# A spiking-rate recommender on one core: last step by pieces, the table's partial part moved forward, two blocks stored in halves, splits finished one copy later

## The chip, the cores and the metric

The kernel runs on one core of one Trainium2 chip. The metric is the time of one execution on the device in microseconds (us). Before the change the median of 3 runs is 1647.41 us (1646.87 to 1650.15). The profile is one further execution, which took 1574.98 us.

## The reference, cut to what matters

A batch of 1024 sequences of 50 item numbers looks up rows of 128 numbers in a table of 100,001 items (row 0 counts as zero). The running mean of the rows is normalised over the batch at each step, drives a leaky spiking unit for 50 steps, and the mean spike count is multiplied by the whole table.

```python
e = emb[seq]                                   # 1024 x 50 x 128
prefix = jnp.cumsum(e, axis=1)
uF = prefix / jnp.minimum(t_idx, lengths)      # t_idx = 1..50
y = (uF - mean) * rsqrt(var + 1e-5) * gamma + beta     # mean, var over the batch
# 50 times: v = v + (x - v)/2; spike = v >= 1; v = v - spike
scores = spikes.mean(axis=0) @ emb.T           # 1024 x 100001, float32
```

The output alone is 1024 x 100,001 x 4 bytes = 409.6 MB.

## The kernel before, in words

**Stage one: 50 steps.** Everything is kept with the 128 features on the partitions and the 1024 sequences along the free axis. GpSimd (POOL) gathers the rows of step t+1 with 8 indirect DMAs of 128 rows each (`gather`, L195). TensorE (PE) transposes the eight blocks of step t into two PSUM banks, `pre[0]` and `pre[1]`, where the running sum builds up (L307). VectorE (DVE) scales each half of 512 columns (L316) and takes its statistics (L317), joins them (L327), and works out the normalising factor in five small instructions (L340 to L346), with a square root on ScalarE (ACT, L331) between. ACT applies the factor (`x`, L350), DVE subtracts half of what is left of the old state (`step`, L353), and PE sums the spikes by a matmul with the identity (`counted`, L275). In the last step (t = 49) the state is made in three groups of 128, 512 and 384 columns (L378), and each group's spikes are added to the count so far (`spiked`, L286), which gives `countA`, `countB` and `countC`, the left operands of stage two. A row of 16 idle transposes (`warm`, L376) keeps PE going meanwhile.

**Stage two: scores.** The table is cut into 98 parts of 1024 items; the last one, part 97, has 673. A part is read as rows (`fetch`, L99), transposed by PE into PSUM (`turned`, L128), and split into a rounded copy `hi` by ACT (L150) and the remainder `lo` by DVE (L151): `prepare`. `product` (L155) multiplies one of eight count blocks n (128 sequences each) with `hi` and `lo`. DVE and ACT take turns at copying the results out of PSUM with the factor 1/50 (L467, L469), and SyncE (SP) stores them (`store`, L167).

The parts are worked on in chunks: `WIDTHS` gives 4 chunks of 2 parts, 4 of 3, 11 of 6 and 3 of 4. Within a chunk, the loop runs over n = 0 to 7 and then over the chunk's parts, so that one pair (chunk, n) is a block that is stored with one DMA, of 1024, 1536, 3072 or 2048 KB. The output tiles `o` have four places in chunks 0 to 3 and three afterwards (`turns`, L432, L436, L440); a block can be written only when the store that last used its place has landed. PSUM holds four tiles of 1024 columns (`ps`, L410), shared by products and transposed parts in order of use.

The next chunk's parts are prepared inside the current one: `ready()` (L445) is called after the blocks n = 2 to 6 (L478) and after each part of block 7 (L475), and prepares one part if there is a place for it. Chunk 0 is special: its block n = 0 is made ahead of the loop (L394 to L404), and its block n = 1 is stored part by part (L471).

The first 38 parts are read in stage one by SP; the others are read by ACT's queue, three parts at a time, in the chunks from number 8 on, after the blocks n = 1 and n = 4 (L481). Part 97 is the last one read there: a DMA of its 5 full groups of 128 rows (L115), 512 bytes to a packet, and one of the 33 rows that are left (L120).

Nothing reorders the program: every engine works in the order in which the code issues. The build gives the DMAs of SP and ACT eight completion semaphores in turn, in the order of the code, and each DMA waits, on the engine that issues it, for the DMA eight before it.

Of the kernel before, what the change touches and what calls it, by code (L numbers as in the profile page):

```python
# [20 lines left out]
P = 128  # L21
# [15 lines left out]
def rec_kernel(  # L37
# [35 lines left out]

    parts = -(-N // HALF)
    assert sum(WIDTHS) == parts
    rows = {}
    split = {}

    free = [
        [embp.tile([P, HALF], F32R, tag=f"{x}{i}", name=f"{x}_{i}") for x in ("hi", "lo")] for i in range(2)  # L80
    ]

    def size(q):
        return min(HALF, N - q * HALF)
# [14 lines left out]
    def fetch(r, q, n):  # L99

        engine = nc.sync if q < HELD else nc.scalar
        k = slot(q)[1]
        n = min(n, parts - q)
        whole = n - (size(q + n - 1) < HALF)
        if whole:
            engine.dma_start(
                out=r[:, k : k + whole, :],
                in_=table[q * HALF : (q + whole) * HALF, :].rearrange("(q p k) d -> p q (k d)", p=P, k=KQ),
            )
        if whole < n:  # L110
            full, rest = divmod(size(parts - 1), P)
            c1 = (parts - 1) * HALF
            r = r[:, k + whole, :].rearrange("p (k d) -> p k d", d=D)
            if full:
                engine.dma_start(  # L115
                    out=r[:, :full, :],
                    in_=table[c1 : c1 + full * P, :].rearrange("(k p) d -> p k d", p=P),
                )
            if rest:
                engine.dma_start(out=r[:rest, full, :], in_=table[c1 + full * P : N, :])  # L120

    def turned(q, pt):
        r = rows.pop(q)
# [18 lines left out]
    def prepare(q, pt):  # L142
        turned(q, pt)
        split[q] = hi, lo = free.pop(0)
        hw = size(q)
        if hw % 2:
            nc.vector.memset(hi[:, hw : hw + 1].bitcast(F32), 0.0)
            nc.vector.memset(lo[:, hw : hw + 1].bitcast(F32), 0.0)
        vp, vh, vl = views(q, pt, hi, lo)
        nc.scalar.copy(vh, vp)  # L150
        nc.vector.tensor_tensor(vl, vp, vh.bitcast(F32), ALU.subtract)  # L151

    def product(po, q, n, k0, kw):  # L155
        kw += kw % 2
        for j, part in enumerate(split[q]):
            nc.tensor.matmul(  # L158
                po[:, :kw],
                lhsT=counts[n],  # L160
                rhs=part[:, k0 : k0 + kw],
                start=j == 0,
                stop=j == 1,
            )
# [5 lines left out]
    with ExitStack() as ph:  # L170
# [23 lines left out]

        def gather(t):  # L195
            es[t] = gp.tile([P, B], F32, tag="e", name=f"e_{t}")
            for n in range(NB):
                nc.gpsimd.indirect_dma_start(  # L198
                    out=es[t][:, n * P : (n + 1) * P],
                    out_offset=None,  # L200
                    in_=table,
                    in_offset=bass.IndirectOffsetOnAxis(ap=idx[:, n, t : t + 1].bitcast(U32), axis=0),
                )
# [81 lines left out]
        def spiked(out, cs, v):  # L285
            nc.vector.scalar_tensor_tensor(out, v, V_TH, count[:, cs], ALU.is_ge, ALU.add)  # L286

        whole = slice(0, B)
        halves = [slice(h * BANK, (h + 1) * BANK) for h in range(B // BANK)]
        v = None  # L290
# [3 lines left out]
        for t in range(T):  # L294
            last = t == T - 1
            if t + 1 < T:
                gather(t + 1)
            e = es.pop(t)
            if last:
                s = lp.tile([P, B], BF16, tag="s", name=f"s_{t - 1}")  # L300
                nc.vector.tensor_single_scalar(s, v, V_TH, ALU.is_ge)
                nc.vector.tensor_tensor(negv, s, v, ALU.subtract)
            uF = up.tile([P, B], F32, tag="uF", name=f"uF_{t}")
            bs = sp.tile([P, B // BANK, 6], F32, tag="bs", name=f"bs_{t}")
            for h, cs in enumerate(halves):
                for k in range(0, BANK, P):
                    nc.tensor.matmul(  # L307
                        pre[h][:, k : k + P],
                        lhsT=e[:, h * BANK + k : h * BANK + k + P],
                        rhs=ident,  # L310
                        start=False,
                        stop=last,
                        is_transpose=True,
                        skip_group_check=True,
                    )
                nc.vector.scalar_tensor_tensor(uF[:, cs], rlen[:, cs], 1.0 / (t + 1), pre[h], ALU.max, ALU.mult)  # L316
                nc.vector.bn_stats(bs[:, h, :], uF[:, cs])  # L317
            if not last:
                correct(t + 1, l)
            else:  # L320

                counted(t - 1, s)
# [4 lines left out]
            nc.vector.bn_aggr(mv, bs.rearrange("p h s -> p (h s)"))  # L327


            r = sp.tile([P, 1], F32, tag="r", name=f"r_{t}")  # L330
            nc.scalar.activation(r, mv[:, 1:2], AF.Sqrt, bias=eps)  # L331
            nc.scalar.activation(uF, uF, AF.Identity, bias=mv[:, 0:1], scale=-1.0)


            if t and not last:
                s = lp.tile([P, B], BF16, tag="s", name=f"s_{t - 1}")
                nc.vector.tensor_single_scalar(s, v, V_TH, ALU.is_ge)  # L337
                counted(t - 1, s)

# [12 lines left out]
            def step(vt, cs):  # L352
                nc.vector.scalar_tensor_tensor(vt, negv[:, cs], -0.5, vt, ALU.mult, ALU.add)  # L353

            if not last:
                vt = vp.tile([P, B], F32, tag=f"v{t % 2}", name=f"v_{t}")
                x(vt, whole)
                if t:
                    nc.vector.tensor_tensor(negv, s, v, ALU.subtract)
# [18 lines left out]
        groups = [  # L378
            (slice(0, P), pre[0][:, :P], countA),
            (slice(P, P + BANK), pre[1], countB),  # L380
            (slice(P + BANK, B), vC, countC),
        ]
# [40 lines left out]
    for c, W in enumerate(WIDTHS):  # L423
# [30 lines left out]
        for n in range(NB):  # L454
# [2 lines left out]
            pool, tag, most = turns[blocks % len(turns)]  # L457
            blocks += 1
            o = pool.tile([P, most * HALF], F32, tag=tag, name=f"o_{c}_{n}")
            for q in range(q0, q1):  # L460
                h0 = (q - q0) * HALF
                hw = size(q)
# [2 lines left out]
                    product(po[:, k0 : k0 + BANK], q, n, k0, min(BANK, hw - k0))  # L465
                if turn % 2 == 0:
                    nc.vector.tensor_scalar_mul(o[:, h0 : h0 + hw], po[:, :hw], 1.0 / T)  # L467
                else:
                    nc.scalar.mul(o[:, h0 : h0 + hw], po[:, :hw], 1.0 / T)  # L469
# [39 lines left out]
```

## Time and profile before

| what | value |
|---|---|
| median of 3 runs | 1647.41 us |
| profiled execution: its time, its span | 1574.98 us, 1573.2 us |
| first gather to end of the last | 4.2 to 503.6 us |
| first store of scores issued | 511.62 us |
| last store of scores issued | 1561.15 us |
| busy: PE, DVE, ACT, POOL | 1147.9, 942.1, 630.6, 378.5 us |
| HBM read, written | 77.69 MB, 409.60 MB |
| mean granted TensorE clock | 0.966 |

A busy time is what an engine spent in its instructions; issuing a DMA doesn't count. The second part of the page cuts the span into 40 slices of 39.3 us and gives the busy share of each engine and of the 16 DMA engines together. The chain of waits follows the run back from its end, at each step to what released it. A group's row gives its line, engine, operation, shapes and count, then the busy time and mean duration, then how long its engine sat idle before it and what ended that. The rows of DMA issues give the median time from issue to landing, which is the time at which the last of the 16 DMA engines has finished its share. The profiled execution is 72.4 us shorter than the median of the runs; no view says where that lies.

### The profile page before, as it was taken

How to read it: one execution, taken by the hardware profiler on the slowest of the kernel's cores; microseconds unless marked ns; L12 is line 12 of the kernel's file. 1: busy time of each engine (PE TensorE's matmuls, PEld its weight loads, DVE VectorE, ACT ScalarE, POOL GpSimd, SP SyncE). 2: the span in 40 equal slices, each digit the busy share in tenths (PEclk: the TensorE clock that was granted, in tenths of full speed). 3: DMA queues.
4: the chain of work that ended last, by engine and by line, in shares of the span. 5: the costliest groups of instructions: out<-in, count | busy, mean ns of one | idle time of the engine just before them, and what ended most of it. 6: DMA issues, size and time to landing. Idle time of an engine off the chain costs nothing.

```text
span 1573.2 us, 12601 instructions
## 1 busy us (share of the span) xinstructions
PE 1147.9 (73%) x4538; PEld 817.6 (52%) x4548; DVE 942.1 (60%) x1161; ACT 630.6 (40%) x700; POOL 378.5 (24%) x406
## 2 busy tenths in 40 slices
PE   4555555555555998889878878887888778777885
PEld 2222222222233776668667666666666667665763
DVE  4777777777777665667555545545555555554553
ACT  2322222222233554555444444444444444443442
POOL 6777777777776000000000000000000000000000
PEclk9999999999999999999999999999999999999998
DMA  9622222222221999999999999999999999999898
GB/s 338 247 53 53 53 53 52 53 53 53 53 79 45 385 416 403 423 417 402 426 429 428 430 427 424 421 415 428 418 428 423 414 428 410 426 424 426 362 423 371
DMA packets 54859, 488.14 MB, mean 310 GB/s; under 512 B 12139, under 2 KB 12940, under 8 KB 32524
## 3 DMA queue, kind: packets, MB, share of 16 engines
q1 hardware_dynamic: 33424, 429.81, 65.1%
q0 software_dynamic: 12800, 26.24, 6.3%
q10 hardware_dynamic: 8572, 31.28, 5.0%
q8 instruction: 36, 0.59, 0.1%
q14 instruction: 27, 0.22, 0.0%
HBM read 77.69 MB, written 409.60 MB: 310 GB/s over the span
## 4 chain that ended last, share of the span: by engine, by line
DMA 50%; POOL 19%; PE 11%; issue 10%; ACT 5%; DVE 4%; another core or an unknown queue 0%; DVEq 0%; ACTq 0%; SPq 0%; POOLq 0%
DMA scores<-o 46%; POOL e L198 19%; PE po L158 10%; ACT o L469 4%; DMA e<-in_L_rec_emb_table,idx 3%; DVE o L467 2%; DMA rows<-in_L_rec_emb_table 2%; PE pt L128 1%; PE pre L307 0%; ACT pairs L150 0%; DVE s L337 0%; DVE bs L317 0%; DVE uF L316 0%; DVE pairs L151 0%; DMA idx<-in_r_seq 0%
## 5 line engine op out<-in xcount | busy, mean ns | idle before, releaser
L467 DVE TENSOR_SCALAR o<-po 128x1024 f32<-128x1024 f32 x391 | 464.1, 1220 | 354.3 <-DMA scores<-o 314.5
L469 ACT ACTIVATE o<-po 128x1024 f32<-128x1024 f32 (+1 forms) x391 | 388.1, 1019 | 548.9 <-DMA scores<-o 336.2
L198 POOL DMA_INDIRECT e<-in_L_rec_emb_table,idx x400 | 377.8, 945 | 124.5 <-issue 116.4
L158 PE MATMUL po<-pairs,countB 128*128 128x512 f32 x1136 | 304.6, 415 | 69.0 <-ACT o L469 52.1
L158 PEld LDWEIGHTS po<-pairs,countB 128*128 128x128 f32 x1136 | 218.5, 197 | 132.0 <-ACT o L469 66.8
L307 PE MATMUL pre<-ident,e 128*128 128x128 f32 x400 | 156.2, 452 | 152.4 <-DMA e<-in_L_rec_emb_table,idx 149.0
L158 PE MATMUL po<-pairs,countC 128*128 128x512 f32 x852 | 230.4, 416 | 49.3 <-ACT o L469 49.3
L158 PEld LDWEIGHTS po<-pairs,countC 128*128 128x128 f32 x852 | 163.6, 198 | 94.2 <-ACT o L469 60.5
L307 PEld LDWEIGHTS pre<-ident,e 128*128 128x128 f32 x400 | 79.2, 200 | 246.1 <-DMA e<-in_L_rec_emb_table,idx 223.6
L151 DVE TENSOR_TENSOR pairs<-pt,pairs 128x1024 fp32r<-128x1024 f32 x71 | 86.3, 1222 | 91.3 <-ACT pairs L150 91.2
L331 ACT ACTIVATE r<-mv,eps 128x1 f32<-128x1 f32 x50 | 14.7, 295 | 305.5 <-DVE mv L327 305.5
L316 DVE SCALAR_TENSOR_TENSOR uF<-rlen,pre 128x512 f32<-128x512 f32 x100 | 68.4, 684 | 108.3 <-PE pre L307 108.2
L128 PE MATMUL pt<-ident,rows 128*128 128x128 f32 x782 | 111.7, 290 | 9.7 <-ACT o L469 5.1
L128 PEld LDWEIGHTS pt<-ident,rows 128*128 128x128 f32 x782 | 100.3, 152 | 29.9 <-issue 8.8
L158 PE MATMUL po<-hi,countB 128*128 128x512 f32 x216 | 89.5, 414 | 15.8 <-ACT o L469 12.6
L264 PE MATMUL pre<-zT,l 128*128 128x512 f32 x100 | 78.1, 783 | 18.9 <-DVE uF L316 18.8
L275 PE MATMUL sums<-s,ident_h 128*128 128x512 bf16 x88 | 45.4, 607 | 60.6 <-DVE s L337 60.6
L158 PE MATMUL po<-lo,countB 128*128 128x512 f32 x216 | 86.5, 402 | 0.0
L158 PE MATMUL po<-pairs,countA 128*128 128x512 f32 x284 | 71.7, 395 | 9.3 <-ACT o L469 9.2
L150 ACT CAST pairs<-pt 128x1024 fp32r<-128x1024 f32 x71 | 71.8, 1012 | 15.0 <-PE pt L128 14.8
L158 PE MATMUL po<-hi,countC 128*128 128x512 f32 (+1 forms) x162 | 67.8, 418 | 11.7 <-ACT o L469 11.7
L350 ACT ACTIVATE v<-uF,hgb,a 128x1024 f32<-128x1024 f32 x49 | 59.2, 1208 | 37.6 <-DVE a L346 37.5
(76 smaller groups left out, 841.9 us busy)
## 6 DMA issues: line engine op xcount, KB each, us to landing
scores<-o SPq DMA_DIRECT2D x88, 3072.0 KB, 20.3
scores<-o SPq DMA_DIRECT2D x32, 1536.0 KB, 8.9
scores<-o SPq DMA_DIRECT2D x16, 2048.0 KB, 12.6
scores<-o SPq DMA_DIRECT2D x30, 1024.0 KB, 8.6
rows<-in_L_rec_emb_table ACTq DMA_DIRECT2D x19, 1536.0 KB, 29.3
rows<-in_L_rec_emb_table SPq DMA_DIRECT2D x6, 3072.0 KB, 25.3
scores<-o SPq DMA_DIRECT2D x8, 1872.5 KB, 11.3
e<-in_L_rec_emb_table,idx POOLq DMA_INDIRECT x400, 2.5
```

The lines of the kernel that those rows point to most:

```text
L128: nc.tensor.transpose(pt[:, k0 : k0 + kw], r[:kw, k0 : k0 + D], ident[:kw, :kw])
L150: nc.scalar.copy(vh, vp)
L151: nc.vector.tensor_tensor(vl, vp, vh.bitcast(F32), ALU.subtract)
L158: nc.tensor.matmul(po[:, :kw], lhsT=counts[n], rhs=part[:, k0 : k0 + kw], start=j == 0, stop=j == 1,)
L198: nc.gpsimd.indirect_dma_start(out=es[t][:, n * P : (n + 1) * P], out_offset=None, in_=table, in_offset=bass.IndirectOffsetOnAxis(ap=idx[: ...
L264: nc.tensor.matmul(pre[h], lhsT=l, rhs=zT[:, h * BANK : (h + 1) * BANK], start=t == 0, stop=False, skip_group_check=True,)
L275: nc.tensor.matmul(sums[h], lhsT=ident_h, rhs=s[:, h * BANK : (h + 1) * BANK], start=t == 0, stop=t == T - 2, skip_group_check=True,)
L307: nc.tensor.matmul(pre[h][:, k : k + P], lhsT=e[:, h * BANK + k : h * BANK + k + P], rhs=ident, start=False, stop=last, is_transpose=True, ...
L316: nc.vector.scalar_tensor_tensor(uF[:, cs], rlen[:, cs], 1.0 / (t + 1), pre[h], ALU.max, ALU.mult)
L350: nc.scalar.activation(vt, uF[:, cs], AF.Identity, bias=hgb[:, 1:2], scale=a)
L467: nc.vector.tensor_scalar_mul(o[:, h0 : h0 + hw], po[:, :hw], 1.0 / T)
L469: nc.scalar.mul(o[:, h0 : h0 + hw], po[:, :hw], 1.0 / T)
```

## The change

**Last step by pieces.** In the last step block 4 (columns 512 to 639) is gathered last, and the step is worked in pieces of 512, 384 and 128 columns instead of two halves. The sums for the earlier spikes (`counted`) move ahead of the last piece's transposes. The old state `negv` is made in three parts, each placed between other work. In all steps one of the five small DVE instructions goes, and another, `ve`, is placed where DVE waits for the square root. `warm` uses the other PSUM tile.

**The partial part.** `order` puts parts 96 and 97 at places 2 and 3, so that they form chunk 1 (1697 columns) and are read in stage one; the last chunk is now 4096 columns wide where it was 3745.

**Halves.** In chunk 8, the first with 6 parts, the blocks n = 0 and 1 are stored after 3 parts and again after 6.

**The split one copy later.** `prepare` no longer issues DVE's subtraction. It is issued by `finish()`, after DVE's next copy out of PSUM, or ahead of a product that needs it. In chunk 0, `ready()` is called from n = 4 on and no longer from n = 2.

```diff
+    order = [0, 1, parts - 2, parts - 1, *range(2, parts - 2)]
...
+    def column(q):
+        return order[q] * HALF
...
         nc.scalar.copy(vh, vp)
-        nc.vector.tensor_tensor(vl, vp, vh.bitcast(F32), ALU.subtract)
+        unsplit.append((q, vp, vh, vl))
+
+    def finish():
+        while unsplit:
+            _, vp, vh, vl = unsplit.pop(0)
+            nc.vector.tensor_tensor(vl, vp, vh.bitcast(F32), ALU.subtract)

     def product(po, q, n, k0, kw):
         kw += kw % 2
+        if any(u[0] == q for u in unsplit):
+            finish()
...
-            for n in range(NB):
+            order = list(range(NB))
+            if t == T - 1:
+                order.append(order.pop(NB // 2))
+            for n in order:
...
+        thirds = [slice(0, P), slice(P, P + BANK), slice(P + BANK, B)]
+
+        def negated(cs):
+            nc.vector.tensor_tensor(negv[:, cs], s[:, cs], v[:, cs], ALU.subtract)
...
-                nc.vector.tensor_tensor(negv, s, v, ALU.subtract)
...
+            pieces = halves if not last else halves[:1] + [slice(B - 3 * P, B), slice(BANK, BANK + P)]
+            bs = sp.tile([P, len(pieces), 6], F32, tag="bs", name=f"bs_{t}")
+            for j, cs in enumerate(pieces):
+                h = cs.start // BANK
+                if last and j == len(pieces) - 1:
+                    counted(t - 1, s)
...
+            ve = sp.tile([P, 1], F32, tag="ve", name=f"ve_{t}")
+            nc.vector.tensor_scalar_add(ve, mv[:, 1:2], BN_EPS)
...
+            if last:
+                negated(thirds[0])
             nc.vector.reciprocal(r, r)
             q = sp.tile([P, 1], F32, tag="q", name=f"q_{t}")
-            nc.vector.tensor_mul(q, r, r)
-            nc.vector.scalar_tensor_tensor(q, mv[:, 1:2], BN_EPS, q, ALU.add, ALU.mult)
+            nc.vector.scalar_tensor_tensor(q, r, ve, r, ALU.mult, ALU.mult)
...
-        warm = vp.tile([P, HALF], F32, tag="v0", name="warm")
+        warm = vp.tile([P, HALF], F32, tag="v1", name="warm")
...
+        negated(thirds[1])
         for cs, vt, _ in groups:
             x(vt, cs)
         cs, vt, first = groups[0]
         step(vt, cs)
         spiked(first, cs, vt)
+        negated(thirds[2])
...
                 if turn % 2 == 0:
                     nc.vector.tensor_scalar_mul(o[:, h0 : h0 + hw], po[:, :hw], 1.0 / T)
+                    finish()
...
-                if c == 0 and n == 1:
-                    store(n, q * HALF, o[:, h0 : h0 + hw])
                 if n == NB - 1:
                     free.append(split.pop(q))
                     ready()
-            if c or n > 1:
-                store(n, q0 * HALF, o[:, : min(N, q1 * HALF) - q0 * HALF])
-            if 2 <= n < NB - 1:
+                if q + 1 == q1 or c == 0 and n == 1 or c == MIDDLE and n < 2 and (q + 1 - q0) % 3 == 0:
+                    store(n, column(q0) + done, o[:, done : h0 + hw])
+                    done = h0 + hw
+            if (2 if c else 4) <= n < NB - 1:
                 ready()
```

`fetch` is rewritten so that it reads neighbouring full parts with one DMA, and the partial one with the two DMAs that it had. The first group of six parts, one DMA before, now takes five: parts 0 and 1, part 96, the two of part 97, and parts 2 and 3.

More of the change, by code (lines that the diff above doesn't have):

```diff
@@ L75, in rec_kernel @@
     assert sum(WIDTHS) == parts
+    order = [0, 1, parts - 2, parts - 1, *range(2, parts - 2)]
     rows = {}
     split = {}
+    unsplit = []
     free = [
@@ L81, in rec_kernel @@
     ]
+    def column(q):
+        return order[q] * HALF
     def size(q):
-        return min(HALF, N - q * HALF)
+        return min(HALF, N - column(q))
     def slot(q):
@@ L101, in fetch @@
         engine = nc.sync if q < HELD else nc.scalar
[L102 to L114, printed above, removed]
+        end = min(q + n, parts)
+        while q < end:
+            k, c0, n = slot(q)[1], column(q), 1
+            if size(q) == HALF:
+                while q + n < end and column(q + n) == c0 + n * HALF and size(q + n) == HALF:
+                    n += 1
                 engine.dma_start(
-                    out=r[:, :full, :],
-                    in_=table[c1 : c1 + full * P, :].rearrange("(k p) d -> p k d", p=P),
-                )
-            if rest:
-                engine.dma_start(out=r[:rest, full, :], in_=table[c1 + full * P : N, :])
+                    out=r[:, k : k + n, :],
+                    in_=table[c0 : c0 + n * HALF, :].rearrange("(q p k) d -> p q (k d)", p=P, k=KQ),
+                )
+            else:
+                full, rest = divmod(size(q), P)
+                part = r[:, k, :].rearrange("p (k d) -> p k d", d=D)
+                if full:
+                    engine.dma_start(
+                        out=part[:, :full, :],
+                        in_=table[c0 : c0 + full * P, :].rearrange("(k p) d -> p k d", p=P),
+                    )
+                if rest:
+                    engine.dma_start(out=part[:rest, full, :], in_=table[c0 + full * P : N, :])
+            q += n
     def turned(q, pt):
@@ L301, in rec_kernel @@
                 nc.vector.tensor_single_scalar(s, v, V_TH, ALU.is_ge)
-                nc.vector.tensor_tensor(negv, s, v, ALU.subtract)
             uF = up.tile([P, B], F32, tag="uF", name=f"uF_{t}")
-            bs = sp.tile([P, B // BANK, 6], F32, tag="bs", name=f"bs_{t}")
-            for h, cs in enumerate(halves):
-                for k in range(0, BANK, P):
+            pieces = halves if not last else halves[:1] + [slice(B - 3 * P, B), slice(BANK, BANK + P)]
[4 more added lines that the diff above has]
+                    counted(t - 1, s)
+                for c0 in range(cs.start, cs.stop, P):
+                    k = c0 - h * BANK
                     nc.tensor.matmul(
                         pre[h][:, k : k + P],
-                        lhsT=e[:, h * BANK + k : h * BANK + k + P],
+                        lhsT=e[:, c0 : c0 + P],
                         rhs=ident,
@@ L315, in rec_kernel @@
                     )
-                nc.vector.scalar_tensor_tensor(uF[:, cs], rlen[:, cs], 1.0 / (t + 1), pre[h], ALU.max, ALU.mult)
-                nc.vector.bn_stats(bs[:, h, :], uF[:, cs])
+                nc.vector.scalar_tensor_tensor(
+                    uF[:, cs],
+                    rlen[:, cs],
+                    1.0 / (t + 1),
+                    pre[h][:, cs.start - h * BANK : cs.stop - h * BANK],
+                    ALU.max,
+                    ALU.mult,
+                )
+                nc.vector.bn_stats(bs[:, j, :], uF[:, cs])
             if not last:
@@ L320, in rec_kernel @@
             else:
-                counted(t - 1, s)
                 count = once.tile([P, B], F32, tag="zT", name="count")
@@ L358, in rec_kernel @@
                 if t:
-                    nc.vector.tensor_tensor(negv, s, v, ALU.subtract)
+                    negated(whole)
                 step(vt, whole)
@@ L377, in rec_kernel @@
         vC = vp.tile([P, B - BANK - P], F32, tag="v1", name="vC")
[L378 to L382, printed above, removed]
+        groups = list(zip(thirds, (pre[0][:, :P], pre[1], vC), (countA, countB, countC)))
+        negated(thirds[1])
         for cs, vt, _ in groups:
@@ L459, in rec_kernel @@
             o = pool.tile([P, most * HALF], F32, tag=tag, name=f"o_{c}_{n}")
+            done = 0
             for q in range(q0, q1):
@@ L467, in rec_kernel @@
                     nc.vector.tensor_scalar_mul(o[:, h0 : h0 + hw], po[:, :hw], 1.0 / T)
+                    finish()
                 else:
```

## The prediction

> **What bounds the kernel now.** I read the page's slices and chain first, then the waits of SP's queue, then the stretches in which the DMA engines are not full, in windows of 1 us.
>
> ```profile
> PE   4555555555555998889878878887888778777885
> DMA  9622222222221999999999999999999999999898
> DMA 50%; POOL 19%; PE 11%; issue 10%; ACT 5%; DVE 4%; another core or an unknown queue 0%; DVEq 0%; ACTq 0%; SPq 0%; POOLq 0%
> L198 POOL DMA_INDIRECT e<-in_L_rec_emb_table,idx x400 | 377.8, 945 | 124.5 <-issue 116.4
> ```
>
> There are two stages. Up to about 504 us POOL issues 400 gathers, 0.945 us each with some 0.3 us between them: 400 x 1.25 = 499 us, without a break. Nothing that DVE saves in the first 49 steps counts, because POOL sets their pace. From 512 us on the DMA engines are full, while PE shows 7 to 9 tenths and DVE (60% of the span) has room too. So the change can gain in three places: between the last gather and the first store, in gaps of the stores, and at the end.
>
> The gaps look like this. The last two columns are the share of the 16 DMA engines and GB/s.
>
> ```profile
> 521.00:522.00 1.00, 1.00 (x6) 0.83 (x5) 1.00 (x2) 0.64 (x1) 0.00 (x0) 1.00 0.07 25
> ...
> 713.00:714.00 1.00, 1.00 (x6) 0.80 (x5) 1.00 (x2) 0.25 (x1) 0.00 (x0) 1.00 0.21 86
> ```
>
> ```profile
> 1457.00:1458.00 1.00, 1.00 (x4) 0.80 (x3) 0.56 (x1) 0.41 (x1) 0.00 (x0) 0.50 0.32 135
> ...
> 1460.00:1461.00 1.00, 1.00 (x6) 0.82 (x5) 0.82 (x2) 0.51 (x1) 0.00 (x0) 1.00 0.09 34
> 1461.00:1462.00 1.00, 1.00 (x11) 0.93 (x9) 0.58 (x1) 0.73 (x1) 0.00 (x0) 1.00 0.04 16
> ```
>
> Added up as 1 minus the share, the gap from 1453 to 1463 is 6.3 us, the one around 713 to 719 about 2 us, and the start (512 to 522) 2.1 us. The big one has a clear cause in SP's waits and in the landing times of the reads:
>
> ```profile
> SPq L167 <- DMA rows<-in_L_rec_emb_table: 26.7, 3, 13.1
> ```
>
> ```profile
> rows<-in_L_rec_emb_table ACTq DMA_DIRECT2D x19, 1536.0 KB, 29.3
> ...
> rows<-in_L_rec_emb_table ACTq DMA_DIRECT2D x1, 320.0 KB, 50.7
> ```
>
> The read of part 97 takes 50.7 us to land where a read of three full parts takes 29.3. Eight completion semaphores go round among SP's and ACT's DMAs, so the store eight DMAs later waits for it, up to 13.1 us, with all later stores behind it on SP.
>
> But a gap in the mean share is not yet lost time. At 1460 to 1462 the share is 0.09 and 0.04, and one engine of 16 is 0.06: about one engine is still working, while the other fifteen have run out. ACT's copies, which start when a store has fully landed, show whether that last engine ever paused:
>
> ```profile
> 1453.79 1.94 ACT L469 ACTIVATE o<-po 128x1024 f32<-128x1024 f32 x2 [5.66 <-DMA scores<-o]
> ...
> 1464.14 1.02 ACT L469 ACTIVATE o<-po 128x1024 f32<-128x1024 f32 x1 [0.94 <-DMA scores<-o]
> ...
> 1469.81 1.94 ACT L469 ACTIVATE o<-po 128x1024 f32<-128x1024 f32 x2 [2.04 <-DMA scores<-o]
> ...
> 1474.89 1.94 ACT L469 ACTIVATE o<-po 128x1024 f32<-128x1024 f32 x2 [1.86 <-DMA scores<-o]
> ```
>
> From 1453.79 to 1474.89, 21.1 us, four stores of 2048 KB land (one of them releases DVE, at 1458.95). Undisturbed, three such stores take 15.2 us (issues at 1487.42 and 1502.59 in the chain), 5.07 each, so four take 20.3. The slowest engine lost at most 0.8 us in a gap of 6.3. At 713 it is the same: ACT's waits for landings at 709.61 and 743.90 are 34.3 us apart, and three stores of 1536 KB (3.86 each, from the waits at 701.87, 705.75 and 709.61) and three of 3072 KB (7.52, from 743.90, 751.39 and 758.95) make 34.1. The stage is bound by one DMA engine that lags behind the others; the gaps are the others waiting for it.
>
> **What the Trainium skill says.** "DMA: Bandwidth & Descriptors", section "Why a DMA increments its semaphore by 16 and not by 1": up to 16 engines finish a DMA independently, and only the full count means that it has landed. The trace agrees: places come free at an even pace although 15 engines idle. The same page, "Queues, rings and completion order": each engine serves its queues in turn, packet by packet. That explains the 50.7 us: many packets of 512 bytes, each behind a long packet of a store. "VectorE: DVE Perf Modes", section "The TRN2 errata": a fixed cost for each instruction. Here a DVE instruction takes 0.30 us on 128 columns, 0.56 on 384 and 0.69 on 512, so that pieces cost more in all but end sooner.
>
> **The change part by part, against the profiled execution (1574.98 us, span 1573.2).**
>
> *Last step.* DVE's rows before:
>
> ```profile
> 506.55 0.69 DVE L317 BATCH_NORM_STATS2 bs<-uF 128x6 f32<-128x512 f32 x1
> 507.28 0.21 DVE L327 BATCH_NORM_AGGREGATE mv<-bs 128x2 f32<-128x12 f32 x1
> ...
> 518.75 1.23 DVE L151 TENSOR_TENSOR lo<-pt,hi 128x1024 fp32r<-128x1024 f32 x1 [1.40 <-ACT hi L150]
> ```
>
> The last gather feeds PE at 505.31; after that 0.67 + 0.69 are needed on 512 columns, in future 0.30 + 0.30 on 128. DVE reaches the last piece at about 506.0, having done 502.13 + 1.22 (spikes) + 0.68 + 0.69 + 0.56 + 0.55 and the pauses, so the aggregate starts at about 506.65: 0.65 earlier. `ve` (0.16) and `negated(thirds[0])` (0.30) exceed the 0.36 wait for the square root by 0.14; one instruction less gives 0.19 back: 0.0. `negated(thirds[1])`, about 0.65, lies in an idle 0.59 ahead of `step`, where only ACT's copies were awaited: 0.13 late. So `countA` and the first store (511.62) come 0.5 earlier. `negated(thirds[2])`, 0.55, stands ahead of `countB`: 0.65 - 0.13 - 0.55 and the pauses leave `countB` 0.1 to 0.2 later than before. Moving `counted` forward (two matmuls, 1.06) fits in PE's wait for the last gather. POOL issues the same 8 gathers. In all other steps POOL's 1.25 x 8 covers everything.
>
> *Chunk 0 without a split at n = 2.* Between its blocks 2 and 3 go eight transposes (1.03), ACT's copy (1.01), and on DVE 1.40 of waiting and 1.23 of subtraction. Block 3's store came at 521.17, 3.3 us after block 2's; without the split PE's 1.85 us for a block sets it, at about 519.3. The gap 521 to 522 (0.93) closes. All engines were idle there, so this is real. With the 0.5 at the first store, less what returns at 515 and 518 because `countB` is no earlier: 1.15 in all (bounds 0.3 and 1.7). The two splits now come at n = 4 and 7, when two stores of 2.5 us are queued.
>
> *Partial part.* The stall goes. Gain for the slowest engine: 0 to 0.8, I take 0.3. Stage two reads 351 more rows, 180 KB, 0.4 us at 420 GB/s, less the dearer small packets: 0.2 lost. Five DMAs for one at the start lie on an SP that is otherwise idle until 444 us; POOL waited 3.0 us in 10 times in all for gathers to land. Chunk 1 writes 351 columns less and the last one more: 0.
>
> *Halves.* PE and DVE deliver the first half 2 us sooner, but the slowest engine did not lack work. Two DMAs of 1536 KB cost 7.72 for 7.52: 0.2 lost for each of two blocks, bounds 0 and 0.4; I take 0.3.
>
> *Split one copy later.* DVE's wait for ACT, 91.3 us over 71 splits, moves behind a copy. The price: a transposed part keeps one of four PSUM tiles longer, and when the copy waits for a place in `o`, the subtraction (1.23) now waits too, and PE with it. In a block with two splits that is some 1.5 us more, against 7.7 from a free place to the store in the longest case (1027.85 to 1035.45). Two more stores of 7.5 us are queued meanwhile, 15 us. So 0. If that cover were gone, every such block would cost up to 1.5.
>
> Sum: -1.15 - 0.3 + 0.2 + 0.3 = -0.95 us. The profile would become 1574.0. The median is 72.4 us above the profiled time, and no view says where; I carry the difference over as it is: 1647.4 - 0.95 = 1646.5 us.
>
> **The rivals.** *The gaps count in full*: 6.0 at 1453, 1.8 at 713, 1.15 at the start, less 0.5: -8.45, 1639.0 us. For it: the share of the page's slices, and the runs may not share the profile's one slow engine. Against it: the even landings. *The last step does not get shorter*, because the last piece waits for PSUM or for `counted`, and the start gains nothing: 0.2, 1647.6 us. *Starved by the later subtraction*: in the 11 chunks of 6 parts, block 7 takes its splits behind its copies. It decides when the path from a free place to the store exceeds the 15 us that are queued; at 0.5 us beyond it, 11 x 0.5 - 0.95 = +4.55, 1652.0 us. Against it: 7.7 + 1.5 is well below 15.
>
> **How the numbers follow.** Forecast 0.57, last step not shorter 0.16, gaps in full 0.19, starved 0.08. About 0.2% (3.3 us) is what a measurement of this kernel can tell from no change. The forecast (bounds 1645 to 1648) and the second rival lie within it; the first rival lies beyond it, from 1644 down to 1637; the last is slower. That gives faster 0.19, same 0.73, slower 0.08. The range 1640.0 to 1649.3 takes in the first two and half of the first rival.
>
> **What would show it.** The first store at about 511.1 and no gap at 521; no wait of SP for rows; after the split's move, longer idle of DVE ahead of L467 but none of the DMA queue. If I am right, the lag persists: the fifteen faster engines idle in small gaps or at the end instead, and the stores land at the same pace. If the landings from 1453 on come 5 us earlier than the start alone explains, the first rival is right. If windows of 1 us show low shares at the end of each chunk of 6 parts, the last is.

## The result, and the profile after

| | median | lowest to highest | runs |
|---|---|---|---|
| before | 1648.26 us | 1646.87 to 1650.15 | 4 |
| after | 1648.68 us | 1646.67 to 1650.16 | 4 |

The ratio is 1.0001, with a 95% interval from 0.9984 to 1.0018: no difference that can be measured. The profiled execution of after took 1650.16 us, its span is 1648.0 us. It can't be laid straight beside the profile of before (1574.98 us), because, as the experiments below suggest, the two come from chips on which stage one takes different times; the record names no chip for either. So I read stage one and stage two separately.

The page of after first: busy shares of PE and granted clock in 40 slices, DMA share, the chain, POOL's gathers.

```profile
PE   4343433334343498988988788887888888887884
PEclk7555555555555589999999989999999999999998
DMA  9511111111112179999999999999999999999998
DMA 38%; PE 19%; DVE 16%; another core or an unknown queue 9%; POOL 6%; ACT 6%; issue 5%; DVEq 0%; ACTq 0%; SPq 0%; POOLq 0%
L217 POOL DMA_INDIRECT e<-in_L_rec_emb_table,idx x400 | 378.6, 946 | 184.6 <-issue 114.3
```

POOL is no longer the chain's second entry (19% before, 6% here). Its gathers cost what they did, but it sits idle for 184.6 us between them instead of 124.5. The last gather starts at 563.5 us instead of 502.7, and the first store is issued at 583.9 instead of 511.6: the 72 us lie in stage one. From the first store to the end it is 1064.1 us here, and 1061.6 in the profile of before. Stage two didn't become shorter, it became longer.

Next the waits of SP's queue (us in total, times, longest): the longest in total, and the only one that a DMA ends:

```profile
SPq L183 <- DVE o L507: 875.4, 176, 11.1
SPq L546 <- DMA scores<-o: 11.8, 3, 4.9
```

The waits for rows (26.7 us before) are gone; what is left is the wait for the last stores at the end. And the windows of 1 us, with the DMA share and GB/s last. The first and third lie as long after the first store as the gaps at 521 and 713 did; the fourth and fifth answer to those from 1457 on:

```profile
593.00:594.00 1.00, 1.00 (x9) 0.92 (x8) 0.12 (x1) 1.00 (x2) 0.00 (x0) 1.00 1.08 451
645.00:646.00 1.00, 1.00 (x3) 0.78 (x3) 0.00 (x0) 0.67 (x1) 0.00 (x0) 0.50 0.08 33
785.00:786.00 1.00, 1.00 (x6) 0.83 (x5) 1.00 (x2) 0.67 (x1) 0.00 (x0) 1.00 1.04 442
1528.00:1529.00 1.00, 1.00 (x6) 1.00 (x5) 0.25 (x1) 0.05 (x1) 0.00 (x0) 0.50 0.23 98
1535.00:1536.00 1.00, 1.00 (x9) 0.91 (x7) 0.00 (x0) 1.00 (x2) 0.00 (x0) 1.00 0.16 66
```

The gaps that the change aimed at are closed (shares 1.08 and 1.04; a little above 1 occurs in this view). In their place stands a new one at 645, with TensorE's clock at 0.50, and gaps late in the stage remain.

### The profile page after: what moved, and what is told of

The parts are those of the page before. It is cut to its first block, busy times and chain, and to the rows that moved or that the text cites. A ratio compares the mean times of both kernels' runs of the same rounds, so it can differ in the third digit from the quotient of the medians.

```text
span 1648.0 us, 12648 instructions
## 1 busy us (share of the span) xinstructions
PE 1114.5 (68%) x4548; PEld 827.3 (50%) x4548; DVE 941.6 (57%) x1165; ACT 636.2 (39%) x700; POOL 379.3 (23%) x406
## 4 chain that ended last, share of the span: by engine, by line
DMA 38%; PE 19%; DVE 16%; another core or an unknown queue 9%; POOL 6%; ACT 6%; issue 5%; DVEq 0%; ACTq 0%; SPq 0%; POOLq 0%
DMA scores<-o 37%; PE po L174 17%; POOL e L217 6%; ACT o L510 5%; DVE bs L356 3%; DVE uF L348 3%; DVE v L393 2%; DVE s L376 2%; DVE negv L311 2%; PE pt L136 2%; DVE o L507 2%; DMA e<-in_L_rec_emb_table,idx 1%; DVE a L386 0%; DVE mv L364 0%
## 5 line engine op out<-in xcount | busy, mean ns | idle before, releaser
L507 DVE TENSOR_SCALAR o<-po 128x1024 f32<-128x1024 f32 x391 | 469.9, 1221 | 475.4 <-DMA scores<-o 326.8
L510 ACT ACTIVATE o<-po 128x1024 f32<-128x1024 f32 (+1 forms) x391 | 394.0, 1020 | 546.0 <-PE po L174 319.1
L217 POOL DMA_INDIRECT e<-in_L_rec_emb_table,idx x400 | 378.6, 946 | 184.6 <-issue 114.3
L174 PE MATMUL po<-pairs,countB 128*128 128x512 f32 x1136 | 308.2, 417 | 74.2 <-ACT o L510 59.6
L283 PEld LDWEIGHTS pre<-zT,l 128*128 128x128 f32 x100 | 27.8, 279 | 289.6 <-issue 176.5
L348 DVE SCALAR_TENSOR_TENSOR uF<-rlen,pre 128x512 f32<-128x512 f32 (+1 forms) x101 | 68.2, 675 | 168.6 <-remote 152.1
L136 PE MATMUL pt<-ident,rows 128*128 128x128 f32 x782 | 108.0, 283 | 12.1 <-ACT o L510 8.3
L339 PE MATMUL pre<-ident,e 128*128 128x128 f32 x400 | 102.7, 422 | 18.4 <-DMA e<-in_L_rec_emb_table,idx 14.3
L136 PEld LDWEIGHTS pt<-ident,rows 128*128 128x128 f32 x782 | 96.3, 147 | 31.3 <-ACT o L510 12.8
L339 PEld LDWEIGHTS pre<-ident,e 128*128 128x128 f32 x400 | 85.5, 223 | 50.9 <-issue 25.3
L294 PE MATMUL sums<-s,ident_h 128*128 128x512 bf16 x98 | 49.6, 608 | 75.4 <-DVE s L376 45.5
```

Source lines behind the costliest of these rows:

```text
L136: nc.tensor.transpose(pt[:, k0 : k0 + kw], r[:kw, k0 : k0 + D], ident[:kw, :kw])
L174: nc.tensor.matmul(po[:, :kw], lhsT=counts[n], rhs=part[:, k0 : k0 + kw], start=j == 0, stop=j == 1,)
L217: nc.gpsimd.indirect_dma_start(out=es[t][:, n * P : (n + 1) * P], out_offset=None, in_=table, in_offset=bass.IndirectOffsetOnAxis(ap=idx[: ...
L283: nc.tensor.matmul(pre[h], lhsT=l, rhs=zT[:, h * BANK : (h + 1) * BANK], start=t == 0, stop=False, skip_group_check=True,)
L294: nc.tensor.matmul(sums[h], lhsT=ident_h, rhs=s[:, h * BANK : (h + 1) * BANK], start=t == 0, stop=t == T - 2, skip_group_check=True,)
L339: nc.tensor.matmul(pre[h][:, k : k + P], lhsT=e[:, c0 : c0 + P], rhs=ident, start=False, stop=last, is_transpose=True, skip_group_check=True,)
```

## The experiments

The runs were made in four groups, each on one chip, which I call A to D. The kernel before was timed along with each group:

| chip | kernel before, median | lowest to highest | runs |
|---|---|---|---|
| A | 1647.76 us | 1639.57 to 1649.27 | 31 |
| B | 1574.88 us | 1574.53 to 1575.82 | 16 |
| C | 1647.73 us | 1639.69 to 1650.00 | 43 |
| D | 1574.62 us | 1574.20 to 1575.39 | 25 |

### Where the 72 us are (chip A)

**The kernel before, unchanged.**

> The kernel before, unchanged, profiled again. Theory A (the 72 us that the first profiled execution lacked are lost in stage one, whatever the change, because TensorE runs there below its full clock in nearly every execution): span about 1645 us, gathers until about 562 us instead of 504, POOL idle about 60 us more than in the first profile, TensorE completing transposes 0.43 us or more apart instead of 0.21. Rival (the change itself lengthened stage one by 60 us and gained as much in stage two): a span of 1645 us with stage one ending at 504 and a longer stage two.

Measured: 1647.87 us, ratio 1.0002 (0.9984 to 1.0020). Its profiled execution has a span of 1647.0 us, the last gather at 563.3, the first store at 584.3. In this respect before and after are alike; the rival falls. The change has nothing to do with the 72 us. One sign that I had named is missing: at a clock of 0.50 the transposes start 0.21 us apart (eight in 1.91 us), not 0.43. Whether TensorE's clock has to do with the 72 us is the next question.

**Idle matmuls** in stage one, to keep TensorE busy, two ahead of each transpose and, in a second kernel, three:

```diff
+            spare = vp.tile([P, B], F32, tag=f"v{t % 2}", name=f"spare_{t}")
...
+                    for _ in range(2):
+                        nc.tensor.matmul(spare[:, :BANK], lhsT=ident_h, rhs=ones, start=True, stop=True)
                     nc.tensor.matmul(
                         pre[h][:, k : k + P],
```

> The kernel after with two idle bf16 matmuls of 512 columns ahead of every transpose in steps 1 to 48, written to a PSUM tile that is dead at that time; outputs unchanged. Theory A1 (TensorE idles too much in stage one, so that its clock is held down; more work lifts it): stage one at POOL's pace, 10.0 us for each step, time about 1577 us. Rival A2 (the clock is held down for another reason, such as a cap on power): 16 x 0.43 = 6.8 us more TensorE work for each step at half clock, stage one longer by 50 us or more, about 1700 us.

> As the run with two, but three idle matmuls ahead of each transpose (24 for each step, 5.1 us at full clock, 10.2 at half). Theory A1: as with two or a little nearer to 1575 us, if two didn't suffice. Rival A2: about 24 x 0.43 = 10.2 us more for each step, 1850 us or more.

Measured: 1687.52 us with two, ratio 1.0255 (1.0217 to 1.0292), and 1770.28 us with three, 1.0757 (1.0718 to 1.0796). Most steps took an even 11.5 to 12.4 us with two and 13.7 us with three. Neither theory had this. The PSUM tile that I used becomes free only when VectorE has read the state of two steps back, so the idle work stood in a row with VectorE's: it waited 45 times for VectorE's `negv`, 60.6 us in all with two and 42.8 with three. I repeated the test without that wait.

**A third place for gathered rows** (`bufs=2` to `bufs=3` in the pool `gather`).

> The kernel after with three places for gathered rows instead of two, so that POOL can run a step further ahead. If stage one is long because a late TensorE holds POOL up now and then (mean speed of TensorE sufficient, only the coupling costs): POOL's pauses shrink, time between 1580 and 1620 us. If TensorE itself is too slow on average in the slow stretches, the pauses stay: within 5 us of 1648.

Measured: 1651.43 us, ratio 1.0029 (1.0019 to 1.0040). POOL sits idle for 185.2 us between its gathers, against 184.6 in the profile of after. More lead for POOL doesn't help: the steps themselves take 11.4 us on average, where POOL needs 10.0.

### The clock is not the cause (chips B and C)

**Zero matmuls that wait for nobody**, one ahead of each transpose and, in a second kernel, two:

```diff
+                    for _ in range(1 if 1 < t < T - 1 else 0):
+                        nc.tensor.matmul(
+                            sums[0], lhsT=zero, rhs=ones, start=False, stop=False, skip_group_check=True
+                        )
```

> The kernel after with one idle bf16 matmul of 512 columns ahead of every transpose in steps 2 to 48, which adds zeros to the count bank that only TensorE touches, so that it waits for no other engine (in the runs with two and three idle matmuls the idle work waited for VectorE each step, and a step grew by 1.7 us, 8 x 0.213, for each matmul more; taken back to one, that line gives 10.3 us a step). Theory A1 (an idle TensorE is what makes the 15 to 18 us steps): steps of 10.0 to 10.3 us without a slow one, stage one shorter by 55 to 65 us, time 1580 to 1595 us. Rival A2 (the 15 to 18 us steps come whatever TensorE does between transposes): 1648 to 1665 us.

> As the run with one zero matmul, but two ahead of each transpose (16 for each step, 3.4 us at full clock, 6.8 us at half). Theory A1: POOL sets the pace at 10.0 us for each step, time 1575 to 1585 us. Rival A2, and also if the waiting for VectorE was not what the earlier dose cost: as the run with two idle matmuls, about 1685 us.

Measured: 1575.83 us and 1579.95 us. It looks like theory A1 at its best, and it is nothing of the kind: these two ran on chip B, where the kernel before takes 1574.88 us too (ratios 1.0006, 0.9997 to 1.0015, and 1.0038, 1.0024 to 1.0052). Without the kernel before at its side the run would have been taken for a gain of 72 us. So I ran the first one again, and got chip C.

> The kernel after with one zero matmul ahead of each transpose, as before, in the hope of a chip where the kernel before takes 1648 us. There, theory A1 (a busier TensorE has no 15 to 18 us steps): about 1576 to 1595 us. Rival A2 (the slow steps belong to the chip and come all the same): 1648 to 1665 us. On a chip where the kernel before takes 1575 us both say 1575 to 1577 us.

Measured: 1647.97 us, ratio 1.0008 (0.9995 to 1.0020). The page shows the clock in stage one at 6 to 7 tenths instead of 5, and the long steps are still there (up to 16.5 us). With one zero matmul ahead of each transpose, theory A1 doesn't hold; the second kernel, with two, ran on chip B alone. A result can also be late at full clock: the last transpose of a step starts at 300.82 us, with the clock at full from 293.8 to 304.0, and VectorE gets it at 309.12. The reverse case stands on chip D: `narrow_only`, told below, ran there with the clock at half throughout stage one. Clock, POOL's gathers and DVE's scaling, first of the kernel before on chip A, then of `narrow_only` on chip D:

```profile
PEclk7555555555555599999999998999989999998998
L198 POOL DMA_INDIRECT e<-in_L_rec_emb_table,idx x400 | 378.4, 946 | 184.5 <-issue 109.1
L316 DVE SCALAR_TENSOR_TENSOR uF<-rlen,pre 128x512 f32<-128x512 f32 x100 | 68.0, 680 | 178.0 <-remote 165.1
```

```profile
PEclk7555555555555999999999999899998999998998
L217 POOL DMA_INDIRECT e<-in_L_rec_emb_table,idx x400 | 377.7, 944 | 124.2 <-issue 111.9
L348 DVE SCALAR_TENSOR_TENSOR uF<-rlen,pre 128x512 f32<-128x512 f32 (+1 forms) x101 | 68.4, 678 | 103.7 <-PE pre L339 103.6
```

The clock row is nearly the same, and yet one takes 11.4 us for a step on average and the other 10.0. Also among the runs of the kernel before on chip D, ten have a mean clock of about 0.81 and a median of 1574.5 us, and those with 0.9 and more have 1574.7. Half clock alone doesn't make the long steps.

What differs is how late TensorE's results reach the others. A long step in the timeline of the kernel before on chip A (start, duration, operation, and in brackets the idle time before it and what ended it):

```profile
296.54 1.91 PE L307 MATMUL pre<-ident,e 128*128 128x128 f32 x8
...
305.98 0.69 DVE L316 SCALAR_TENSOR_TENSOR uF<-rlen,pre 128x512 f32<-128x512 f32 x1 [6.77 <-remote]
306.70 0.69 DVE L317 BATCH_NORM_STATS2 bs<-uF 128x6 f32<-128x512 f32 x1
306.81 0.76 PE L264 MATMUL pre<-zT,l 128*128 128x512 f32 x1 [8.36 <-issue]
308.86 0.69 DVE L316 SCALAR_TENSOR_TENSOR uF<-rlen,pre 128x512 f32<-128x512 f32 x1 [1.47 <-PE pre L264]
309.09 0.95 POOL L198 DMA_INDIRECT e<-in_L_rec_emb_table,idx  x1 [3.71 <-PE pre L264]
```

and a step of `narrow_only` on chip D:

```profile
323.72 0.48 PE L339 MATMUL pre<-ident,e 128*128 128x128 f32 x1 [0.87 <-DMA e<-in_L_rec_emb_table,idx]
324.90 0.47 PE L339 MATMUL pre<-ident,e 128*128 128x128 f32 x1 [0.71 <-DMA e<-in_L_rec_emb_table,idx]
...
325.42 0.69 DVE L348 SCALAR_TENSOR_TENSOR uF<-rlen,pre 128x512 f32<-128x512 f32 x1 [2.34 <-PE pre L339]
```

On chip D, DVE starts 0.52 us after the start of the last transpose that it needs. On chip A all eight transposes have started by 298.1, and DVE gets the first four only at 305.98; POOL, which needs their buffer, waits until 309.09. The "remote" in brackets means that the trace found no event to credit. TensorE's semaphore events in this stretch come 2.1 to 2.8 us apart (298.26, 301.07, 303.17, 305.95), where in the next step they come 0.21 us apart (313.11, 313.32, 313.54). Most such steps, of 15 to 20 us, follow one or two of 7.5 us.

One thing about this does depend on what TensorE does, and it stands in the two kernels with idle matmuls, on the same chip A. In steps 2 to 47 of the kernel before there, VectorE's first scaling starts over 3 us, and up to 14, after the last transpose that it needs in 19 of 46 steps. With two idle matmuls ahead of each transpose it never starts more than 0.5 us after it, with three 0.4; the waits of the scaling are no longer "remote" but for the transposes:

```profile
L355 DVE SCALAR_TENSOR_TENSOR uF<-rlen,pre 128x512 f32<-128x512 f32 (+1 forms) x101 | 68.8, 681 | 209.8 <-PE pre L346 108.2
```

With one zero matmul, on chip C, it is up to 8.6 us again. So the late results went away with 16 idle matmuls in a step and stayed with 8 (the two sorts of kernel also differ in the tile that they write). The time was no shorter, because idle work and VectorE's in a row took 11.4 us and more for each step. Whether 16 that wait for nobody would bring a chip like A or C nearer to 1575 us was not run.

Why results come late on chips A and C, and not on B and D, stays open: neither the granted clock alone nor the number of gather buffers decides it. Each chip was used for one group of runs, so it is not known either whether a chip keeps its kind.

### The parts of the change (chips C and D)

**After, once more, on chip C.**

> The kernel after, unchanged, once more, since the time of the kernel before has turned out to depend on the chip (1647.8 us on one, 1574.9 us on another, 72.9 us apart in stage one). Forecast: 0.95 us less than the kernel before on the same chip, on either kind. Rival (the gaps count in full): 8.5 us less. Rival (later subtraction starves the stores): 4.5 us more.

Measured: 1648.35 us, ratio 1.0014 (1.0001 to 1.0027): at the edge of slower, and in no case 0.95 us faster. From the first store to the end: 1064.6 us.

**The last step alone** (order, whole stores, immediate subtraction and the splits from n = 2 on as in the kernel before; the diff is against the kernel after):

```diff
-    order = [0, 1, parts - 2, parts - 1, *range(2, parts - 2)]
+    order = list(range(parts))
...
         unsplit.append((q, vp, vh, vl))
+        finish()
...
-                if q + 1 == q1 or c == 0 and n == 1 or c == MIDDLE and n < 2 and (q + 1 - q0) % 3 == 0:
+                if q + 1 == q1 or c == 0 and n == 1:
...
-            if (2 if c else 4) <= n < NB - 1:
+            if 2 <= n < NB - 1:
```

> The kernel before with the last step by pieces and the shorter chain of small VectorE instructions alone: the order of the parts, the whole stores, the immediate subtraction and the splits from n = 2 on are those of before. Forecast: first store 0.5 us earlier, time 0.5 us less than before. Rival (the last step does not get shorter): 0. If the slowest DMA engine alone sets stage two, the whole 0.5 us must show at the end; if something else sets the end, less.

Measured: 1646.02 us, ratio 0.9993 (0.9983 to 1.0003); 1061.5 us from the first store to the end. The interval doesn't tell 0.5 us from nothing. On chips A and C the first store itself moves by several us from run to run, since a long step may or may not fall at the end of stage one.

**After without the later subtraction** (only the second hunk above).

> The kernel after with VectorE's subtraction issued at once again (all else as after, the splits in chunk 0 from n = 4 on too). Forecast: the same as the kernel after within 0.3 us, because VectorE's 91 us of waiting for ScalarE lie beside full DMA queues. If the later subtraction costs (PSUM kept longer), this kernel is faster than after by 0.5 us or more; if it gained, slower by as much.

Measured: 1646.17 us, ratio 0.9998 (0.9984 to 1.0012); 1061.9 us from the first store. The forecast said equal to after within 0.3; it is 2.2 us below after on the same chip. Part of that can be the end of stage one, which moves there, but the later subtraction is a suspect, and the traces say where. The share of the DMA engines that is missing in the stretch from 40 to 80 us after the first store, in chunks 1 to 3, is 2.8 us in after (3.0 in after, once more) and 0.2 us in this kernel. This kernel and the last step alone differ by the partial part, the halves and the later splits in chunk 0; their times, 1646.17 and 1646.02 us, show no gain of these three together, and no run tells them apart. Two last kernels put this to the test; the second has `c >= NARROW` in the condition.

```diff
                 to_split += 1
+                if c < NARROW:
+                    finish()
```

> The kernel after, but in chunks 0 to 3 (2 parts each) the subtraction is issued at once; from chunk 4 on it stays one copy later. Seven profiles of kernels with the later subtraction take 1062.6 to 1066.4 us from the first store to the end, and those without it 1061.5 to 1062.7; 40 to 80 us after the first store, in chunks 1 to 3, the DMA engines miss about 3 us with it and 0.2 us without. Theory N (the cost is in the narrow chunks): at most 0.5 us missing in that stretch, 1061 to 1062 us from the first store to the end, time 2 us less than the kernel after. Rival W (my forecast's third rival: the cost is in the wide chunks): 1063.5 us or more from the first store, time as the kernel after.

> The kernel after with the subtraction one copy later in chunks 0 to 3 alone, at once from chunk 4 on. Theory N: about 3 us missing 40 to 80 us after the first store, 1063.5 to 1065 us from the first store to the end, 2 us more than the kernel with the later subtraction in the wide chunks alone. Rival W: at most 1062 us, 2 us less than that kernel.

Measured, both on chip D: 1574.32 us (ratio 0.9998, 0.9989 to 1.0006) with the later subtraction in the chunks from 4 on, and 1575.86 us (1.0008, 1.0000 to 1.0017) with it in chunks 0 to 3. That is 1.5 us apart; from the first store to the end it is 1062.0 and 1063.7 us. Theory N holds, and rival W falls. One size is well below what I expected: in the stretch from 40 to 80 us, `narrow_only` misses 1.2 us where I had written 3. The nine profiles with the later subtraction in chunks 0 to 3 miss between 1.2 and 3.0 us there, with the same code in these chunks, so a single figure says little. From the first store to the end these nine take 1062.6 to 1066.4 us, and the five without it there 1061.5 to 1062.7. The rates of 40 us each from the first store on, of `wide_only` and then of `narrow_only` (DMA share and GB/s last):

```profile
511.33:551.33 40.00, 37.36 (x179) 29.21 (x178) 26.87 (x27) 19.73 (x23) 0.00 (x0) 1.00 0.97 392
551.33:591.33 40.00, 34.91 (x167) 27.24 (x166) 24.39 (x21) 19.92 (x20) 0.00 (x0) 1.00 1.00 410
```

```profile
510.19:550.19 40.00, 34.83 (x167) 27.31 (x166) 25.25 (x26) 18.71 (x22) 0.00 (x0) 0.98 0.95 384
550.19:590.19 40.00, 37.67 (x173) 30.40 (x171) 24.50 (x21) 20.66 (x21) 0.00 (x0) 0.93 0.97 399
```

(8 + 11) GB/s x 40 us = 0.76 MB less, 1.8 us at 415 GB/s, and 1.7 us is what `narrow_only` takes longer. `wide_only` is the best version here, but its 0.3 us to before can't be told from nothing.

## Why the prediction was right, and the step of it that failed

The verdict (no difference) and the range were right, and the median of 1648.7 us lies 2.2 us above the 1646.5. Against the kernel before as timed beside it, 1648.26 us, it is 0.4 us more, and the interval reaches from 2.6 less to 3.0 more. So the result alone can't judge terms of 1 us; the runs of the parts must. The working, step by step:

**POOL sets the pace of stage one.** This holds on chips B and D (10.0 us a step) and not on A and C (11.4). What I drew from it came true on both, on A and C for another reason than mine: in the first 49 steps one VectorE instruction less, 0.19 us each, 9 us in all, moved nothing. The last gather starts at 563.3 us in the kernel before on chip A, and at 563.5 and 563.3 in two profiles of after.

**The 72.4 us carried over as a constant.** Right as a number, and by luck. The reason, which no view of the one profile could give, is in all likelihood that it came from a chip of the kind of B and D (its steps take 10.0 us), and the timed runs from one of the kind of A and C. Had the kernel after been timed on the other kind, where `zero_one` and `narrow_only` take about 1576 us, the forecast would have been 70 us off.

**The last step, 0.5 us.** From the start of the last gather to the first store it was 502.69 to 511.62, 8.93 us. On chips B and D it is now 8.07 (`zero_one`), 8.39 (`wide_only`) and 7.99 (`narrow_only`): 0.5 to 0.9 us less. Right. (`zero_two` took 11.10, with two more matmuls ahead of each transpose up to the step before.)

**The gap at 521, 0.65 of the 1.15.** It closed as forecast. I called it real because all DMA engines were idle there; but the end didn't come earlier for it. In after itself the first 40 us after the first store carry no more than before (384 GB/s, 388 before): the later subtraction opened other gaps there. `wide_only`, without it, has 392, and still takes 1062.0 us from the first store, where the kernel before takes 1061.6, and on chip A 1062.7. With differences of 1 us between profiles of one kernel I can only say that a gain in stage two is not seen.

**The partial part and the halves.** SP no longer waits for rows, and the gap at 713 is filled; the end is no earlier, as forecast. The rival of the gaps in full (8.45 us less) is refuted by all of these runs. The engines that idle less in the middle idle at the end: the share in the last 8 us of the span was 0.41 before, and 0.10 in after. This fits the lag of one DMA engine that I had inferred, but no view shows a single engine. Nor does any run test why the read of part 97 took 50.7 us.

**The split one copy later, 0.** This is the step that failed: it costs about 1.5 us, by `wide_only` and `narrow_only`. On chip D `narrow_only` is 1.2 us above the kernel before, where my sum was 0.95 below; of these 2.2 us, 1.5 are this step, and the 0.65 us not seen is the rest. The kernel after itself was not timed on a chip like B or D. I had the mechanism (when the copy waits for a place in `o`, the subtraction waits too, and TensorE with it) and its price, but I tested the cover only in the chunks of six parts, where two stores of 7.5 us are queued. In chunks 0 to 3 a store of 1024 KB takes 2.5 us, and two of them are gone in 5. The third rival was the right mechanism in the wrong place. The timeline of after at the end of chunk 2:

```profile
638.00 1.22 DVE L507 TENSOR_SCALAR o<-po 128x1024 f32<-128x1024 f32 x1 [1.28 <-DMA scores<-o]
639.06 0.51 PE L174 MATMUL po<-hi,countA 128*128 128x512 f32 x1 [0.39 <-ACT o L510]
640.50 1.22 DVE L507 TENSOR_SCALAR o<-po 128x1024 f32<-128x1024 f32 x1 [1.27 <-DMA scores<-o]
641.64 1.22 DVE L165 TENSOR_TENSOR lo<-pt,hi 128x1024 fp32r<-128x1024 f32 x1
642.90 0.80 PE L174 MATMUL po<-lo,countA 128*128 128x512 f32 x1 [3.34 <-DVE lo L165]
643.50 0.63 PE L174 MATMUL po<-hi,countA 128*128 128x512 f32 x1
...
646.30 1.22 DVE L507 TENSOR_SCALAR o<-po 128x1024 f32<-128x1024 f32 x1 [3.45 <-PE po L174]
```

ScalarE had `hi` ready at 637.54. Issued at once, the subtraction would have followed the copy of 638.00, which ends at 639.22. Now it stands behind one copy more, which waits until 640.50 for a store to land. TensorE waits 3.34 us for `lo`, and the clock is at half: the product takes 0.63 us instead of 0.39, for 6.8 us (641.4 to 648.2). So the store after the one at 639.30 is issued at 645.69, and the share of 0.08 at 645 is the result. TensorE's waits for `lo` (us, times), in after and then in `wide_only`; the view counts matmuls and weight loads apart, so that six are three stalls:

```profile
  DVE lo L165: 14.3, 6
```

```profile
  DVE lo L165: 5.6, 6
```

As many stalls, but longer ones. The matmuls alone waited 6.7 us in after and 6.3 in `narrow_only`, and 2.3 in `wide_only` and 1.7 in the kernel before. I had written that no gap of the DMA queue would follow.

A fall of the clock after pauses is what the Trainium skill describes in "TensorE: Matmul & The Clock Gate", section "HAM oscillation — how this bites in real kernels": pauses of TensorE of more than about 3.4 us bring it back to half clock. The traces agree only in kind. Here the clock fell at 641.35, when TensorE had stood still for 1.8 us. In the fourteen profiles it changes in steps of 3.41 us, and of its 692 falls only 42 had a pause of 3.4 us in the two steps before; in the median the longest pause was 2.0 us, and TensorE was busy for 0.35 of the last step. So shorter pauses are enough, and the measurement decides. What I would have drawn from the same section for stage one, that half clock explains the 72 us, the runs refute.

## What to carry to other kernels

When an instruction is moved behind another one, test the cover where the queued work is shortest, not where the stage spends most of its time; here the blocks of 1024 KB decided, not those of 3072. Time the old kernel beside the new one on the same chip, and ask first whether a profile and the times that it is to explain belong together. A closed gap in the mean share of the DMA engines need not be a gain: here the gaps around 713 and 1453 us shrank, and the end came no earlier.

## What the runs showed of the hardware that was not expected

- Of four chips, two take 1574.9 and 1574.6 us for the same kernel, and two 1647.8 and 1647.7 us. The whole difference lies in stage one, where in every second or third step TensorE's results reach VectorE 3 to 14 us after the last transpose that it needs, and POOL late too; in the profiles from chips B and D, and in the first profile of before, it is at most 2.4 us.
- On chip A the late results were gone with 16 or 24 idle matmuls in a step, and on chip C they were there with 8. Why is open.
- TensorE fell to half clock after pauses of about 2 us: in the median of 692 falls it had been busy for 0.35 of the 3.41 us before. Where full clock stayed, it had been busy for at least 0.43.
- TensorE at half clock through stage one cost nothing on chip D: 1574.5 us at a mean of 0.81, 1574.7 us at 0.9 and more.
- On chips A and C the end of stage one falls on a long or a short step by chance. In the profile of the kernel without the later subtraction the last two steps took 7.6 and 9.2 us (first store at 578.2), in that of after, once more, 17.5 and 9.2 (583.5). The runs of the kernel before there spread from 1639.6 to 1650.0 us, on B and D from 1574.2 to 1575.8.
